# Output projection of the attention layer: three lumps of three products, or nine single products

## The chip, the cores and the metric

The kernel runs on one core of a Trainium2 chip. The metric is the device time of one execution in microseconds (us). The kernel before was timed three times: 6641.83, 6641.19 and 6638.29 us, a median of 6641.19. One further execution was profiled; it took 6638.09 us.

The engines are called TensorE (PE in the profile; PEld is its weight load), VectorE (DVE), ScalarE (ACT), GpSimd (POOL) and SyncE (SP, which issues nearly all DMAs).

## The reference

Four images of 384 channels and 64 x 64 pixels, all in fp32, pass two residual layers. The first is a selective state space layer (not touched here). The second is attention in which every pixel looks at a 7 x 7 window:

```python
qkv = einsum('oc,bchw->bohw', w_qkv, x) + b_qkv          # 12 heads of 32 channels
q, k, v = (qkv[:, 0] * scale, qkv[:, 1], qkv[:, 2])
logits = stack([sum_c q * k_pad[..., di:di+H, dj:dj+W] for di, dj in 7 x 7]) + rel_bias
attn = softmax(logits, axis=-1)
out = einsum('bnhwk,bnkchw->bnchw', attn, v_win).reshape(B, C, H, W)
out = einsum('oc,bchw->bohw', w_proj, out) + b_proj      # the output projection
x = x + out
```

The change concerns the last product alone, 384 x 384 weights on the 512 pixels of a stripe at a time.

## The kernel before

The state space layer fills the first 5145 us. While it runs, its idle engine time also makes keys, queries and values of the first images for the attention layer and stores them in DRAM (`kdr`, `qdr`, `vdr`). Which stripes have theirs is fixed when the program is built: stripes 0 to 14 have keys, queries and values, stripes 15 to 21 have values alone, stripes 22 to 31 nothing.

The attention layer (`attention_layer`, from line 1197) cuts each image into 8 stripes of 8 rows, 32 stripes in all. A stripe (512 pixels) is 12 units (`UNITS`): 4 pairs of 8 x 8 blocks, times 3 groups of four heads. The loop at line 1473 walks over the units `s` and writes out the work of four units in flight, in this order:

- what a piece of the unit before left over (`waiting`: mostly the eviction of its PSUM bank `mm`);
- `keep(s-4)`, every third unit: ScalarE copies a finished pair out of the bank `ov` into `aT`;
- `divide(s-1)`: reciprocal of the sums (`rs`, VectorE) and the product with it (`sg`, GpSimd);
- `scores(s)`: 8 products `lg` on TensorE into four banks, then for each head a bias-add with its row minimum on VectorE (`mx`) and an exponential on ScalarE;
- `turn(s-2)`: 8 transposes `pt` into two banks, one copied out by VectorE, the other by ScalarE (`pT`);
- the pieces of other stripes: keys, queries and values of stripe + 2 where they aren't in DRAM, and the output projection of stripe - 1 (`project`);
- `weigh(s-3)`: 16 products `ov` of the turned weights with the values `vw`.

After these come DMAs and small work: `load_res` at unit 0 (three loads of the residual into `o`), `load_keys` (three loads `kt`, one `q`) at unit 0, `surround` (four copies of key edges on GpSimd) at units 4, 6 and 8, and the values of a pair, four loads `vw`, after every third unit (2, 5, 8, 11).

Nothing is reordered: the class `Written` (lines 146 to 167) ties each engine's instructions to the order in which the program writes them, SyncE's DMAs included. Every engine and its queue goes through its list in order and waits on semaphores where data or a buffer isn't ready.

All pieces use the one bank `mm`. The projection (line 1334) makes the channel block `m` of a stripe by three products that add up in `mm`; in the unit after, VectorE adds bias and residual into `o` and SyncE stores it. `o` has three buffers, one per block: a load of the next residual block waits for the store of the block before it. Before the change, `pieces` (line 1366) puts the blocks at units 5, 7 and 9 of the following stripe.

In the profile one fp32 product shows as two passes (two MATMUL and two LDWEIGHTS rows).

Of the kernel before, what the change touches and what calls it, by code (L numbers as in the profile page):

```python
# [10 lines left out]
ALU = mybir.AluOpType  # L11
# [3 lines left out]
P = 128  # L15
C = 384
NJ = C // P
# [104 lines left out]
TX = 512  # L122
# [8 lines left out]
RB, CB = 8, 8  # L131
QB = RB * CB
NBLK = HW // CB
NPAIR = NBLK // 2
UNITS = NPAIR * NJ
# [35 lines left out]
def two_layers(  # L171
# [36 lines left out]
    for base, sign in ((0, 1), (GSZ - 1, -1)):  # L208
        nc.gpsimd.affine_select(
            out=grp,  # L210
# [9 lines left out]
    for base, sign in ((0, 1), (GSZ - 1, -1)):  # L220
        nc.gpsimd.affine_select(
            out=grpT,
# [974 lines left out]
    def attention_layer(eng, gm1, qkb, pjb, early, mv):  # L1197
        te, ve, se, ge, dq = eng
        scale = HD**-0.5
        stripes = NB * NXT  # L1200
        with ExitStack() as es:
# [5 lines left out]
            pjv = wt.tile([P, NJ], F32, name="pjv")  # L1207
            bias = early["bias"]
            w_pj = wt.tile([P, NJ, C], F32, name="w_pj")
# [10 lines left out]
            def ring(shape, tag, bufs, k):  # L1220

                if tag not in rings:
                    rings[tag] = list(early.get(tag, ()))
                    for i in range(len(rings[tag]), bufs):
                        rings[tag].append(sb.tile(shape, F32, name=f"{tag}{i}"))
                return rings[tag][k % bufs]

            def of(s):
                return s // NXT, s % NXT
# [11 lines left out]
            def at_of(s):  # L1241
                return ring([P, NJ, TX], "aT", 2, s)
# [45 lines left out]
            def load_keys(s, key_queue):  # L1288
                if s > 0:
                    load_stripe_keys(key_queue, kt_of(s), s)  # L1290
                    load_stripe_queries(dq, q_of(s), s)
# [34 lines left out]
            def o_of(s, m):  # L1326
                return ring([P, TX], "o", NJ, NJ * s + m)

            def load_res(s):
                b, r = of(s)  # L1330
                for m in range(NJ):
                    dq.dma_start(o_of(s, m), x1s[b][m * P : (m + 1) * P, r * TX : (r + 1) * TX])

            def project(s, m, ps):
                b, r = of(s)
                o = o_of(s, m)
                for j in range(NJ):
                    te.matmul(
                        ps, w_pj[:, j, m * P : (m + 1) * P],
                        at_of(s)[:, j, :].rearrange("p (b r c) -> p r b c", b=NBLK, r=RB),  # L1340
                        start=(j == 0), stop=(j == NJ - 1),
                    )
                yield
                ve.scalar_tensor_tensor(o, ps, pjv[:, m : m + 1], o, ALU.add, ALU.add)
                dq.dma_start(out[b, m * P : (m + 1) * P, r * TX : (r + 1) * TX], o)

            def output_bias(ps):

                for m in range(NJ):
                    for j in range(NJ):  # L1350
                        te.matmul(
                            ps[:, m : m + 1], w_pj[:, j, m * P : (m + 1) * P],
                            qkb[:, 2 * NJ + j : 2 * NJ + j + 1],
                            start=(j == 0), stop=(j == NJ - 1),
                        )
                ve.tensor_tensor(pjv, ps[:, :NJ], pjb, ALU.add)

            def has_values(s):
                b, r = of(s)
                return (b, NPAIR * r) in have_values  # L1360

            def has_keys(s):
                b, r = of(s)
                return (b, 2 * r) in have_keys and (b, 2 * r + 1) in have_keys

            def pieces(s, k):

                found = []
                t = s + 1
                if 0 <= t < stripes and not has_keys(t) and k == 0:  # L1370
                    found.append((query, t, 2))
                t = s + 2
                if 0 <= t < stripes:
                    if has_keys(t):
                        table = {}
                    elif has_values(t):
                        table = {2: (key, 0), 4: (key, 1), 6: (key, 2), 10: (query, 0), 11: (query, 1)}
                    else:
                        table = {
                            0: (value, 0), 1: (value, 1), 2: (value, 2), 3: (value, 3),  # L1380
                            4: (key, 0), 6: (key, 1), 8: (key, 2), 10: (query, 0), 11: (query, 1),
                        }
                    if k in table:
                        f, i = table[k]
                        found.append((f, t, i))
                t = s - 1
                if 0 <= t < stripes and k in (5, 7, 9):
                    found.append((project, t, (k - 5) // 2))
                return found

# [37 lines left out]
            def divide(u):  # L1428
                sg, sm, rs = sg_of(u), few_of("sm", u), few_of("rs", u)
                ve.reciprocal(rs, sm)  # L1430
                ge.tensor_tensor(sg, sg, rs.unsqueeze(2).broadcast_to([P, 4, NK]), ALU.mult)

            def turn(u):
                sg, pT = sg_of(u), pt_of(u)
                for c in range(NCH):
                    for hh in range(4):
                        te.transpose(
                            pts[c][:KN, hh * P : (hh + 1) * P],
                            sg[:, hh, c * KN : (c + 1) * KN], ident,
                        )  # L1440
                ve.tensor_copy(pT[:KN, 0, :], pts[0][:KN, :])
                se.copy(pT[:KN, 1, :], pts[1][:KN, :])
# [17 lines left out]
            def keep(u):  # L1460
                s, p, m = where(u)
                se.copy(
                    at_of(s)[:, :, p * P : (p + 1) * P],
                    ov[:, : NJ * P].rearrange("p (m q) -> p m q", m=NJ),
                )


            N = stripes * UNITS
# [1 line left out]
            last_stats = stats_phases(  # L1470
                (te, ve, se.activation, ge, lambda t: None), mv, gm1[NB - 1], lambda: mm, "b3"
            )
            for s in range(-3 * UNITS, N + 12):
                stripe, k = s // UNITS, s % UNITS
                for f in waiting:
                    next(f, None)
                waiting = []
                if s == 4:
                    output_bias(mm)
                if s > 4 and last_stats:  # L1480
                    last_stats.pop(0)()
                if 0 <= s - 4 < N and (s - 4) % NJ == NJ - 1:
                    keep(s - 4)
                if 0 <= s - 1 < N:
                    divide(s - 1)
                if 0 <= s < N:
                    scores(s)
                if 0 <= s - 2 < N:
                    turn(s - 2)
                mine = pieces(stripe, k)  # L1490
                for n, (f, t, i) in enumerate(mine):
                    ps = mm if s >= 0 else (mm, *lgs)[(s + n) % 5]
                    if n == 1 and 0 <= s - 3 < N:
                        weigh(s - 3)
                    g = f(t, i, ps)
                    next(g)
                    if n < len(mine) - 1:
                        next(g, None)
                    else:
                        waiting.append(g)  # L1500
                if len(mine) < 2 and 0 <= s - 3 < N:
                    weigh(s - 3)
                if k == 0 and 0 <= stripe - 1 < stripes:
                    load_res(stripe - 1)
                if 0 <= stripe + 2 < stripes and has_keys(stripe + 2):
                    if k == 0:
                        load_keys(stripe + 2, se if s < 0 else dq)
                    if k in (4, 6, 8):
                        surround(stripe + 2, (k - 4) // 2)
                t = stripe + 2  # L1510
                if 0 <= t < stripes and not has_values(t) and k in (6, 7, 8):
                    pad_values(dq, *of(t), k - 6)
                if k == 2 and 0 <= stripe + 3 < stripes and not has_keys(stripe + 3):
                    load_x(stripe + 3)
                if s == 3 - UNITS:
                    dq.dma_start(w_pj, proj_wT.rearrange("(k p) m -> p k m", p=P))
                if s == 2 * UNITS:
                    dq.dma_start(w_qkv, qkv_wT.rearrange("(k p) m -> p k m", p=P))
                if 6 <= k < 6 + NJ and 0 <= stripe + 3 < stripes and not has_keys(stripe + 3):
                    gn(stripe + 3, k - 6)  # L1520
                pair = (s + 1) // NJ + 1
                if (s + 1) % NJ == 0 and 0 <= pair < stripes * NPAIR:
                    load_pair_values(dq, vw_of(pair), pair)
# [3 lines left out]
    ]  # L1527
    dq = engines[-1]
    attention_layer(engines, *state_space_layer(engines))


# [44 lines left out]
```

## Time and profile before

| | |
|---|---|
| median of three executions | 6641.19 us (6638.29 to 6641.83) |
| the profiled execution, its own time | 6638.09 us |
| its span in the profile | 6636.4 us |
| attention layer, first score product to the end | 5145.1 to 6636.4 us |
| TensorE, VectorE, ScalarE, GpSimd busy in the span | 94%, 88%, 85%, 86% |
| stripes 2 to 12 (5219.27 to 5623.88 us): TensorE, VectorE, ScalarE, GpSimd busy | 386.2, 279.8, 324.1, 230.9 of 404.6 us |
| granted TensorE clock in these stripes | 1.00 |

The span is the time between the first and the last instruction of one execution; its own time holds a little around it. In the profile a line names the engine, the operation, the output tile, an arrow and the inputs (buffer numbers left out), shapes and a count. All lines bear L154, the line of the helper that writes the instructions, so groups are told apart by tile. A line of the view of waits names who waited, the releaser that came last, the total, how often and the longest. The ends of matmuls are modelled, so a high busy share of TensorE doesn't say that it has no idle time; starts are measured.

### The profile page before, as it was taken

The page shows a single profiled execution, that of the slowest core. Times are in us where ns is not written, and L with a number is a line of the kernel's source. Part 1 is how long each engine was busy: PE and PEld are TensorE (multiplying, and loading weights), DVE is VectorE, ACT ScalarE, POOL GpSimd, SP SyncE. Part 2 cuts the span into 40 slices and gives each one's busy share as a digit, 9 for nine tenths or more (in the row PEclk, how much of TensorE's full clock was granted, in tenths as well). Part 3 has the DMA queues.
Part 4 walks back from the last instruction along what each step waited for, and adds up shares of the span by engine and source line. Part 5 has one row for each costly group of instructions (what it writes and reads, how often), then busy time and mean ns, then how long its engine had stood idle before and what let it go on. Part 6 is the DMA issues. An engine that isn't in the chain of part 4 may idle for free.

```text
span 6636.4 us, 133738 instructions
## 1 busy us (share of the span) xinstructions
PE 6220.8 (94%) x47526; PEld 4267.2 (64%) x47526; DVE 5838.6 (88%) x10102; ACT 5612.0 (85%) x14147; POOL 5679.2 (86%) x3032
## 2 busy tenths in 40 slices
PE   6888888988999999999999999999997999999999
PEld 4666666666666666667666766676765555555555
DVE  4999999999999999999999999999998666555555
ACT  4888888888999999999999999999996778665556
POOL 3999999999999999999999999999999555444443
PEclk9999999999999999999999999999998999999999
DMA  5242423233444535353544434353533545223332
GB/s 187 89 131 89 137 91 131 84 130 101 148 153 131 164 119 166 121 174 118 168 133 139 151 124 153 123 166 120 167 110 92 172 151 158 95 94 108 102 101 93
DMA packets 783228, 859.99 MB, mean 130 GB/s; under 512 B 194976, under 2 KB 703024, under 8 KB 782384
## 3 DMA queue, kind: packets, MB, share of 16 engines
q1 hardware_dynamic: 779440, 850.65, 39.9%
q8 instruction: 377, 6.18, 0.4%
q14 instruction: 291, 2.38, 0.1%
q10 hardware_dynamic: 3120, 0.79, 0.1%
HBM read 745.54 MB, written 110.81 MB: 129 GB/s over the span
## 4 chain that ended last, share of the span: by engine, by line
DVE 32%; PE 32%; ACT 25%; issue 5%; POOL 4%; DMA 2%; SPq 0%; POOLq 0%; DVEq 0%; ACTq 0%
DVE h L154 28%; PE mm L154 19%; ACT da L154 8%; PE yps L154 5%; PE pt L154 4%; POOL h L154 3%; ACT sg L154 3%; ACT L154 3%; PE ov L154 2%; PE lg L154 2%; ACT dt L154 2%; ACT sz L154 2%; DVE xn L154 1%; DMA w_in<-wdr 1%; ACT pT L154 1%
## 5 line engine op out<-in xcount | busy, mean ns | idle before, releaser
L154 DVE TENSOR_TENSOR_SCAN h<-da,h 128x373 f32<-128x373 f32 (+1 forms) x4224 | 3616.5, 913 | 62.6 <-ACT da L154 54.0
L154 POOL TENSOR_TENSOR h<-h,BC 128x1488 f32<-128x1488 f32 (+1 forms) x1056 | 3259.8, 3104 | 45.0 <-ACT state L154 41.5
L154 ACT ACTIVATE da<-dt,nega 128x372 f32<-128x372 f32 (+1 forms) x4224 | 2378.9, 571 | 304.6 <-DVE h L154 270.8
L154 POOL TENSOR_TENSOR h<-dtx,BC 128x372 f32<-128x372 f32 (+6 forms) x1056 | 1756.2, 1684 | 42.7 <-ACT dtx L154 34.1
L154 PE MATMUL yps<-ident,h 128*124 128x128 f32 (+1 forms) x12672 | 1601.6, 279 | 121.7 <-POOL h L154 118.2
L154 PEld LDWEIGHTS yps<-ident,h 128*124 128x124 f32 (+1 forms) x12672 | 1456.1, 142 | 335.1 <-POOL h L154 211.5
L154 PE MATMUL mm<-xn,w_in 128*128 128x372 f32 (+3 forms) x3168 | 1091.6, 484 | 77.7 <-DMA w_in<-wdr 28.8
L154 POOL TENSOR_TENSOR sg<-sg,rs 128x784 f32<-128x784 f32 x384 | 574.1, 1495 | 638.3 <-DVE rs L154 510.9
L154 ACT ACTIVATE sg<-sg,mx 128x196 f32<-128x196 f32 x1536 | 685.2, 448 | 385.7 <-DVE mx L154 377.3
L154 DVE TENSOR_TENSOR h<-dtxps,BC 128x1488 f32<-128x1488 f32 (+6 forms) x792 | 967.3, 1235 | 1.3 <-ACT dtx L154 1.3
L154 PEld LDWEIGHTS mm<-xn,w_in 128*128 128x128 f32 x3168 | 571.7, 190 | 413.6 <-DVE h L154 56.8
L154 PE MATMUL mm<-xb,cw 128*128 128x372 f32 (+1 forms) x2112 | 700.1, 477 | 24.7 <-ACT xc L154 19.1
L154 DVE CUSTOM_DVE_ANT_0 sg<-lg,bias 128x196 f32<-128x196 f32 x1536 | 464.4, 358 | 179.7 <-PE lg L154 178.4
L154 PEld LDWEIGHTS mm<-xb,cw 128*128 128x128 f32 x2112 | 393.2, 189 | 287.9 <-ACT xc L154 38.9
L154 ACT ACT_TABLE_LOAD x441 | 565.8, 1283 | 8.4 <-PEq L1561 0.8
L154 PE MATMUL mm<-yg,w_out 128*128 128x372 f32 (+1 forms) x1584 | 526.8, 478 | 0.0
L154 PE MATMUL pt<-ident,sg 128*98 128x128 f32 x3072 | 446.8, 281 | 29.6 <-ACT pT L154 22.1
L154 PEld LDWEIGHTS pt<-ident,sg 128*98 128x98 f32 x3072 | 313.9, 128 | 182.3 <-issue 78.7
L154 PEld LDWEIGHTS mm<-yg,w_out 128*128 128x128 f32 x1584 | 289.0, 191 | 153.3 <-issue 2.3
L154 PEld LDWEIGHTS ov<-pT,vw 98*32 98x32 f32 x12288 | 189.6, 110 | 193.3 <-issue 136.0
L154 ACT ACTIVATION_READ_ACCUMULATOR sg<-sg,mx 128x1 f32 x1536 | 287.8, 187 | 0.0
L154 PE MATMUL mm<-xp,w_qkv 128*128 128x512 f32 x612 | 279.5, 593 | 0.0
(136 smaller groups left out, 7103.5 us busy)
## 6 DMA issues: line engine op xcount, KB each, us to landing
BC<-bcrows SPq DMA_DIRECT2D x320, 744.0 KB
w_in<-wdr SPq DMA_DIRECT2D x528, 192.0 KB
vw<-vdr SPq DMA_DIRECT2D x512, 147.0 KB
cw<-ddr SPq DMA_DIRECT2D x264, 256.0 KB
xs<-in_x_dram SPq DMA_DIRECT2D x210, 186.0 KB
wk<-in_qkv_wT_dram SPq DMA_DIRECT2D x180, 192.0 KB
o<-x SPq DMA_DIRECT2D x96, 256.0 KB
out_dram<-o SPq DMA_DIRECT2D x96, 256.0 KB
```

The lines of the kernel that those rows point to most:

```text
L154: ins = made(*args, **kw)
```

## The change

The new `project_part(s, i, ps)` makes one of the nine products of a stripe (block `i // 3`, term `i % 3`). Where it is the last term of its block, the eviction and the store follow in the next unit, as before. In `pieces` the nine parts go to units 3 to 11 of the following stripe, but only where the two stripes after it need no key, query or value products in this loop (they have keys in DRAM, or don't exist). Elsewhere `project` still runs whole at units 5, 7 and 9; it is now written by way of `project_part`. The stripes during which the new form is used are 1 to 12 and 31, and the tail after the last stripe. The loop is one step longer, so that the last eviction is written.

The eviction of the blocks moves from units 6, 8 and 10 to units 6, 9 and the next stripe's unit 0; the stores move with them. The third store then stands on SyncE behind the values of unit 11 and straight ahead of the residual loads of the next stripe.

```diff
+            def project_part(s, i, ps):
+
+                m, j = divmod(i, NJ)
+                te.matmul(
+                    ps, w_pj[:, j, m * P : (m + 1) * P],
+                    at_of(s)[:, j, :].rearrange("p (b r c) -> p r b c", b=NBLK, r=RB),
+                    start=(j == 0), stop=(j == NJ - 1),
+                )
+                yield
+                if j == NJ - 1:
+                    b, r = of(s)
+                    o = o_of(s, m)
+                    ve.scalar_tensor_tensor(o, ps, pjv[:, m : m + 1], o, ALU.add, ALU.add)
+                    dq.dma_start(out[b, m * P : (m + 1) * P, r * TX : (r + 1) * TX], o)
+
             def project(s, m, ps):
-                b, r = of(s)
-                o = o_of(s, m)
-                for j in range(NJ):
-                    te.matmul(
...
+                for j in range(NJ - 1):
+                    next(project_part(s, NJ * m + j, ps))
+                yield from project_part(s, NJ * m + NJ - 1, ps)
...
                 t = s - 1
-                if 0 <= t < stripes and k in (5, 7, 9):
+                if all(u >= stripes or has_keys(u) for u in (s + 1, s + 2)):
+                    if 0 <= t < stripes and k >= 3:
+                        found.append((project_part, t, k - 3))
+                elif 0 <= t < stripes and k in (5, 7, 9):
                     found.append((project, t, (k - 5) // 2))
                 return found
...
-            for s in range(-3 * UNITS, N + 12):
+            for s in range(-3 * UNITS, N + 13):
```

More of the change, by code (lines that the diff above doesn't have):

```diff
@@ L1332, in load_res @@
                     dq.dma_start(o_of(s, m), x1s[b][m * P : (m + 1) * P, r * TX : (r + 1) * TX])
-            def project(s, m, ps):
-                b, r = of(s)
-                o = o_of(s, m)
-                for j in range(NJ):
-                    te.matmul(
[L1339 to L1345, printed above, removed]
+            def project_part(s, i, ps):
[11 more added lines that the diff above has]
+                    dq.dma_start(out[b, m * P : (m + 1) * P, r * TX : (r + 1) * TX], o)
+            def project(s, m, ps):
+                for j in range(NJ - 1):
+                    next(project_part(s, NJ * m + j, ps))
+                yield from project_part(s, NJ * m + NJ - 1, ps)
             def output_bias(ps):
```

## The prediction

> **What bounds the kernel now.** The stretches by time came first: the last 1491 us of the 6636.4 us span, from 5145, are the attention stage, 32 stripes of 12 units. I took the start of the first score product (`lg`) of every unit. Stripes 2 to 12 last 36.74 to 36.76 us each (stripe 8: 37.12), stripe 1 37.23, stripes 14 to 19 about 50, 20 to 29 about 56.9. The diff touches the projections made during stripes 1 to 12, stripe 31 and the tail: elsewhere a following stripe still needs keys.
>
> TensorE's order of time in stripe 9 (start, length, engine, operation):
>
> ```profile
> 5481.95 0.60 PE L154 MATMUL lg<-kt,q 32*64 32x196 f32 x16
> 5482.48 1.38 PE L154 MATMUL pt<-ident,sg 128*98 128x128 f32 x8
> 5483.80 0.65 PE L154 MATMUL ov<-pT,vw 98*32 98x64 f32 x32
> 5484.38 0.60 PE L154 MATMUL lg<-kt,q 32*64 32x196 f32 x16
> ...
> 5489.44 0.60 PE L154 MATMUL lg<-kt,q 32*64 32x196 f32 x16
> 5489.98 1.39 PE L154 MATMUL pt<-ident,sg 128*98 128x128 f32 x8
> 5491.20 2.74 PE L154 MATMUL mm<-aT,w_pj 128*128 128x512 f32 x6
> 5493.87 0.65 PE L154 MATMUL ov<-pT,vw 98*32 98x64 f32 x32
> 5494.46 0.60 PE L154 MATMUL lg<-kt,q 32*64 32x196 f32 x16
> ```
>
> From `lg` to `lg` a plain unit takes 2.43 us, the first projecting unit 5.02 = 2.44 + 2.58. The 12 starts of a stripe are spaced 2.43, 2.62, 2.44, 2.43, 2.62, 5.02, 2.12, 5.13, 2.12, 5.13, 2.12, 2.56. So 2.12 us is what TensorE needs alone, when nothing it waits for is late, and 2.43 to 2.62 is what something else allows. The chain of waits says what:
>
> ```profile
> 5461.51 2.58 PE mm L154 x6
> 5464.08 0.58 PE ov L154 x32
> ...
> 5476.68 0.98 ACT sg L154 x4
> 5477.65 0.47 ACT pT L154
> 5478.12 0.38 ACT aT L154
> 5478.50 0.58 ACT sg L154 x3
> ```
>
> In projecting units the chain runs over TensorE; in plain units over ScalarE (exponentials, then a copy of the turned weights). The loop is: first bias-add on VectorE, 0.41 us later the first exponential, 1.78 us for four, reciprocal and next bias-add 0.24: 2.43. The waits of 5219 to 5624 us show both sides (columns: who for whom, total us, times, longest):
>
> ```profile
> ACT sg L154 <- DVE mx L154: 58.8, 35, 2.7
> ...
> PEld pt L154 <- ACT pT L154: 43.0, 99, 0.5
> ```
>
> ScalarE stands idle up to 2.7 us in 33 projecting units because TensorE is late; TensorE waits up to 0.5 us in 99 others because ScalarE is late. The two bounds alternate: each lump of 2.58 us stops ScalarE, and the time is not got back.
>
> **What the Trainium skill says.** "TensorE: Matmul & The Clock Gate" (Part 3, "What overlaps and what doesn't") has matmuls finish strictly in program order, so what stands behind a projection waits for it; the trace agrees: `ov` starts 0.95 us after the projection's last weight load, never earlier. "Perfetto Trace Analysis" (Per-instruction lifecycle) calls matmul ends estimates; the trace agrees (rows of 592 ns start 0.43 us apart), so I use starts alone. "PSUM — Partial Sum Buffer" (The four PSUM rules) says that a group's first product clears the flags of its whole bank: a group may stay open over three units only if nothing else starts one there; in these stripes `mm` has no other user. "DMA: Bandwidth & Descriptors" (Anatomy of one DMA) puts any wait of a transfer on the issuing sequencer; SP's own waits show this (100.9 us for `ov`, 69.7 for `rs`, up to 4.5 at once, in the same stretch), and it matters below.
>
> **The change part by part.** No product, eviction or DMA is added or removed: 9 products (18 passes), 3 evictions and 3 stores per stripe move.
>
> *The products.* Six passes cost 2.58 us where TensorE alone binds (4.70 = 2.12 + 2.58 in the units of stripe 15). Passes start 0.427 us apart, so 6 x 0.427 = 2.56 and at most 0.02 us belongs to entering and leaving the group. The value products (three of 384 columns) add 1.94 = 6 x 0.32 + 0.02: the same. One product: 2 x 0.427 + 0.02 = 0.87 us. The trace has no lone product between `pt` and `ov`; bounds of its fixed part: 0 (gone in overlap; not less, since the passes already stream without a gap) to 0.1 us (a further weight wait); I take 0.02.
>
> *Period of a unit with one product.* 2.12 + 0.87 = 2.99 us if nothing else binds. Checked against each engine: ScalarE's loop 2.43, with the `aT` copy 2.62: covered by 0.37. The second half of `pt` needs its bank freed by ScalarE's copy. With `lg` at 0, the bias-add starts at 0.71 (as after every projecting unit), exponentials end at 2.90, copy at 3.5; the next unit wants it at 2.99 + 1.03 = 4.0: 0.5 us of cover. POOL's multiply starts 0.5 after `lg`, lasts 1.5, is needed at 3.5. VectorE's eviction (0.75 us, queued ahead of reciprocal and bias-add) starts 0.5 us before the next `lg` and ends 0.27 after it, while the bias-add waits for `lg` until 0.71: free, and if that cover went, 3 x at most 0.3 us a stripe. The next group's first product waits for this eviction; it comes 1.66 after `lg`, so 1.4 us of cover.
>
> *A stripe.* Units 3 to 11 carry one product. Unit 0 follows a relaxed unit: 2.12. Unit 1: 2.54, the second after it, as 2.56 follows 2.12 now. Unit 2: 2.43. Unit 3, still on ScalarE's bound: 2.43 + 0.87 = 3.30; its product also needs the `aT` copy, which ends 1.60 after `lg` where the product wants 1.66: 0 to 0.1. Units 4 to 11: 8 x 2.99 = 23.92. Sum 34.31, against 36.75: 2.44 less.
>
> *All stripes.* Stripes 2 to 12 now sum to 404.63; 11 x 34.31 = 377.41: 27.2 less. Stripe 1 has no relaxed start: 2.56 + 2.62 + 2.44 + 3.30 + 23.92 = 34.84 against 37.23: 2.4. Stripe 13 begins after a relaxed unit: 0.4. Stripe 31: eleven units from 34.18 to 2.43 + 2.62 + 2.43 + 3.30 + 7 x 2.99 = 31.7, 2.5; unit 11's product there lies under the wait for the last exponentials, perhaps 0.1 more. The tail has the same order on every engine: 0. Sum 32.6 us.
>
> *SP.* The third store now falls after unit 11, straight before the loads of the next residual, and the load into the same buffer must wait until that store has landed; behind it in SP's queue stand the keys, the queries and the values. Now:
>
> ```profile
> 5476.69 3.19 SPq L154 DMA_DIRECT2D vw<-vdr  x4
> 5479.94 1.40 SPq L154 DMA_DIRECT2D o<-x  x3
> 5481.38 5.09 SPq L154 DMA_DIRECT2D kt<-kdr  x3
> 5486.51 0.78 SPq L154 DMA_DIRECT2D q<-qdr  x1
> ```
>
> The first key load is issued 4.5 us after the stripe's start and its sixteen completions are in at 10.8 (9.9 to 12.3 over the stripes). POOL copies from it in unit 4, at 12.7. After: store issued at 3.1, behind the values in the queues, landed at 7.5 to 8.4 (the residual load issued at 3.0 lands there now); key load at 8 to 9; landing, over queues that have emptied, some 3.3 us later: 11.5 to 12.5. POOL wants it at 10.4 (start of unit 4) + 2.0 = 12.4, and has another 2 us before its next multiply is missed by `pt`. Cost 0; to 1 us a stripe if landing takes as long as now (6.3: 15). Values asked for in unit 2 are needed in unit 9, 27.7 us after the start; now they are in by 18.5, so 4 us later does no harm, but in stripe 2, behind the 1.7 MB of `w_qkv`, they now land at 23.7: 0 to 2 us once. I take 0.6 in all.
>
> The sum, 32.0, is taken from the profiled execution: 6638.1 us, span 6636.4, to 6606.1 and 6604.4. The median of the runs shown is 3.1 us above that execution, so 6641.2 - 32.0 = 6609.
>
> **Rivals.** (a) *Part of it is eaten*: keys late on POOL by 1 to 1.5 us beyond its cover, or 0.1 us of fixed cost per product (9 x 0.08 = 0.7 us a stripe): 9 to 18 us lost, 6618 to 6627. For it: SP's queue is the one resource that gets a new wait. Against: the cover above. (b) *No change*: the product adds to ScalarE's period instead of filling its hole, 2.43 + 0.87 = 3.30 in all nine units; 9 x 3.30 + 7.1 = 36.8 a stripe, 6641. For it: the first projecting unit does just this (5.02). Against: after one such unit the wait is gone (2.12). (c) *Slower*: the new store-then-load wait. At 1:1 it must cost over 2.44 us a stripe to turn the sign, that is, key landing beyond 12.4 + 2 + 2.4 = 16.8, 6 us later than now. If the store's receipt took 8 us instead of 4.4 to 5.3, and the keys as long as now: landing near 18, 12 x 1.2 = 14 us slower, 6655. Against: stores on quieter queues land in 2.8 to 4.8 us. (d) *It gains more*: no waits are left on TensorE anywhere in these stripes: 12 x 2.12 + 9 x 0.87 = 33.3, 1 us a stripe better: 6597. Against: units 1 to 3 have no product to cover ScalarE.
>
> **How the numbers follow.** Forecast 77 in 100; (a) 12; (b) 4; (c) 4; (d) 3. The forecast's own range: fixed part 0 to 0.04, `aT` 0.1, `w_qkv` 0 to 2: 6605 to 6614. To leave no more than 2 in 10 outside it takes in half of (a): 6603 to 6621. A measurement of this kernel can tell about 0.2% (13 us) from no change: forecast, (d) and nearly all of (a) are faster, (b) the same, (c) slower: 0.91, 0.05, 0.04.
>
> **What would show it.** Starts of `lg` 2.99 us apart in units 4 to 11 of stripes 1 to 12, 3.30 in unit 3, 2.12 in unit 0; stripes of 34.3; ScalarE's waits on `mx` short and many instead of 2.7 us long; TensorE's waits on `pT` gone but for units 1 to 3; the key copies on POOL not waiting for DMA. Stripes 14 to 30 as before. It is wrong if the spacing is 3.3 (b), or if POOL waits for `kt` and the units after 4 stretch (a, c).

## The result, and the profile after

Median 6608.76 us (6603.49 to 6610.65, six runs) against 6640.41 for the kernel before (six runs in all): ratio 0.9952, 95% interval 0.9939 to 0.9965, so 32 us or about 0.5% faster. The forecast was 6609. The profiled execution took 6608.67 us, its span 6607.0 against 6636.4.

The span fell by 29.4 us. The attention layer, from its first score product to the end, fell from 1491.3 to 1459.3 us, by 32.0; the state space layer, in which the program is the same, happened to last 2.6 us longer in this execution (5147.7 us against 5145.1).

The spacing of the score products `lg`, unit by unit, in a stripe of the middle (stripe 9), worked out from the starts in the trace:

```
unit      0     1     2     3     4     5     6     7     8     9    10    11    stripe
before  2.44  2.62  2.43  2.44  2.62  5.01  2.12  5.12  2.12  5.13  2.12  2.56   36.75
after   2.12  2.55  2.44  3.29  2.99  2.98  2.98  2.98  2.98  2.98  2.98  2.99   34.27
```

TensorE's order of time in stripe 9 of the changed kernel (start, length, engine, operation) has one product (two passes) between the transposes and `ov` of every unit from 3 on:

```profile
5470.06 0.60 PE L154 MATMUL lg<-kt,q 32*64 32x196 f32 x16
5470.59 1.08 PE L154 MATMUL pt<-ident,sg 128*98 128x128 f32 x8
5471.50 1.02 PE L154 MATMUL mm<-aT,w_pj 128*128 128x512 f32 x2
5472.46 0.65 PE L154 MATMUL ov<-pT,vw 98*32 98x64 f32 x32
5473.04 0.59 PE L154 MATMUL lg<-kt,q 32*64 32x196 f32 x16
```

The eight transposes follow each other without a break (1.08 us; 1.38 in the plain units before, where the second four waited for ScalarE). The chain of work that ended last, in the same stripe, stays on TensorE from unit 4 on:

```profile
5471.66 0.86 PE mm L154 x2
5472.53 0.58 PE ov L154 x32
5473.11 0.53 PE lg L154 x16
5473.64 1.01 PE pt L154 x8
5474.65 0.86 PE mm L154 x2
```

The four pieces sum to 2.98 us, the unit's whole length. And the waits in stripes 2 to 12 (who for whom, total us, times, longest):

```profile
ACT sg L154 <- DVE mx L154: 50.2, 98, 1.0
...
PEld pt L154 <- ACT pT L154: 12.9, 33, 0.5
...
POOL kt L154 <- DMA kt<-kdr: 5.2, 9, 1.2
```

Before, ScalarE waited 35 times, up to 2.7 us, and the weight loads of the transposes waited for ScalarE 99 times, 43.0 us in all. Now ScalarE waits 98 times and never over 1.0 us, and the transposes wait for ScalarE 33 times, three a stripe. Counted by unit in stripes 2 to 11, they fall in units 1, 2 and 3 alone; before, they fell in units 0 to 5, 7, 9 and 11, that is, in all but those that follow a lump. The last line is new: GpSimd now waits for keys. It is followed up below.

### The profile page after: what moved, and what is told of

It reads as the page before. It is cut to its first block, busy times and chain, and to the rows that moved or that the text cites. A ratio compares the mean times of both kernels' runs of the same rounds, so it can differ in the third digit from the quotient of the medians.

```text
span 6607.0 us, 133726 instructions
## 1 busy us (share of the span) xinstructions
PE 6202.4 (94%) x47526; PEld 4262.0 (65%) x47526; DVE 5841.8 (88%) x10102; ACT 5612.8 (85%) x14147; POOL 5679.8 (86%) x3032
## 4 chain that ended last, share of the span: by engine, by line
PE 34%; DVE 32%; ACT 22%; issue 5%; POOL 4%; DMA 2%; SPq 0%; POOLq 0%; DVEq 0%; ACTq 0%
DVE h L154 28%; PE mm L154 19%; ACT da L154 8%; PE pt L154 5%; PE yps L154 5%; POOL h L154 4%; ACT L154 3%; PE ov L154 3%; PE lg L154 2%; ACT dt L154 2%; ACT sz L154 2%; ACT sg L154 2%; DMA w_in<-wdr 1%; DVE xn L154 1%; ACT xD L154 1%
## 5 line engine op out<-in xcount | busy, mean ns | idle before, releaser
L154 PE MATMUL pt<-ident,sg 128*98 128x128 f32 x3072 | 431.6, 280 | 14.0 <-ACT pT L154 8.5
```

Of the source, the lines that this page charges most:

```text
L154: ins = made(*args, **kw)
```

## The experiments

The theory: in these stripes TensorE needs 2.12 us a unit and ScalarE's loop 2.43 to 2.62. While TensorE works on the projection, ScalarE gets ahead, so that in the next unit TensorE doesn't wait for it: 0.31 to 0.50 us are saved, once. That holds for a lump (three products in one unit, 2.58 us) and for a single product (0.87 us) alike, so nine singles save nine waits a stripe and three lumps three. The rivals: the gain comes from the new places of evictions, stores and loads; each entry into a projection costs or saves something by itself; the new wait on SyncE eats part of the gain.

All stripe times below are medians of stripes 2 to 11, from the starts of `lg`. Each variant ran once, but for the one with halves, and the first layer, in which the program is the same, ended anywhere from 5143.9 to 5150.1 us; so the stripes decide, not the whole time.

### Lumps at the places of the change

```diff
-                    if 0 <= t < stripes and k >= 3:
-                        found.append((project_part, t, k - 3))
+                    if 0 <= t < stripes and k in (5, 8, 11):
+                        found.append((project, t, (k - 5) // 3))
```

> The changed kernel, but in the stripes concerned each output block is again made by three products in one unit, now at units 5, 8 and 11, so that evictions, stores and residual loads keep the places that the change gave them. Theory (a lump of 2.58 us stops ScalarE, single products fill TensorE's waits): units 5.0 us with a lump, 2.12 and 2.54 after it, about 36.5 us a stripe, nearly as before (36.75), time about 6638. Rival 1 (the gain comes from where VectorE's evictions and the stores went): about 34.3 us a stripe, as in the changed kernel, time about 6609.

Measured: 6640.46 us beside 6640.01 for the kernel before; 36.56 us a stripe. (About 6638 was expected; the attention layer started 3.0 us later than in the profile of the kernel before.) Stripe 9, TensorE:

```profile
5494.23 2.74 PE L154 MATMUL mm<-aT,w_pj 128*128 128x512 f32 x6
5496.90 0.65 PE L154 MATMUL ov<-pT,vw 98*32 98x64 f32 x32
5497.48 0.60 PE L154 MATMUL lg<-kt,q 32*64 32x196 f32 x16
...
5499.65 0.59 PE L154 MATMUL lg<-kt,q 32*64 32x196 f32 x16
...
5502.15 0.60 PE L154 MATMUL lg<-kt,q 32*64 32x196 f32 x16
```

After the lump one short unit (2.17 here, 2.12 as a rule), then 2.50, and ScalarE is the bound again. With evictions, stores and loads where the change has them, but lumps, 0.19 of the 2.48 us a stripe is gained. The first rival is out.

### Two and one

```diff
-                    if 0 <= t < stripes and k >= 3:
-                        found.append((project_part, t, k - 3))
+                    if 0 <= t < stripes and 5 <= k <= 10:
+                        found.append((project_two if k % 2 else project_part, t, (k - 5) // 2 * NJ + 2 * (1 - k % 2)))
```

`project_two` makes two products of a block in one unit.

> The nine products of a stripe as two and one, at units 5 and 6, 7 and 8, 9 and 10: six groups instead of three or nine. Theory: the unit with the first two products 4.16 us, later ones 3.85 (2.12 + 1.73), those with one 2.99, the unit after the last 2.12; about 35.6 us a stripe, that is, half of the gain, time about 6626. Rival 1 (places of evictions and stores, which differ by one unit from those before): about 36.7. Rival 2 (each entry into the projection has a fixed cost that the profile before did not show, so that more groups cost more): above 36.7 us.

Measured: 6627.51 us (before: 6640.01); 35.58 a stripe; the units from 5 to 11: 4.15, 2.99, 3.84, 2.98, 3.84, 2.99, 2.12. The expectation was met to 0.02 us. Six groups are not dearer than three: above TensorE's own 2.12 us, one product costs 0.86, two cost 1.72 and three 2.58 (4.70 = 2.12 + 2.58), so entering a projection has no cost that can be seen.

### Short exponentials, before and after

In both kernels:

```diff
-                        sg[:, hh, :], sg[:, hh, :], AF.Exp, scale=-1.0,
+                        sg[:, hh, KN // 2 : KN + KN // 2], sg[:, hh, KN // 2 : KN + KN // 2], AF.Exp, scale=-1.0,
```

The kernel before with this edit:

> The kernel before, with the exponentials over 98 of the 196 columns (the rest keep the biased logits: half of the softmax is left out), so that ScalarE's loop of a unit shrinks from 2.43 to about 2.13 us, close to TensorE's 2.12. Theory: plain units 2.12 to 2.35, and the lumps cost little more than their length: about 34.0 us a stripe in stripes 2 to 12. Rivals (a cost of the lumps that has nothing to do with ScalarE): the stripe is longer than the same kernel with single products by the full 2.4 us.

The changed kernel with it:

> The changed kernel with the same short exponentials (half of the softmax is left out). Theory: 33.4 to 33.6 us a stripe, units with a product still 2.98; the difference to the kernel before with short exponentials falls from 2.45 us a stripe to about 0.5, and in the whole time from 32 to about 6 us. Rivals: the difference stays 2.4 us a stripe.

Measured: 6593.35 and 6585.80 us. Stripes 33.97 and 33.44 us: the difference between lumps and singles fell from 2.48 to 0.53. The units of stripe 10, with short exponentials in both kernels:

```
unit      0     1     2     3     4     5     6     7     8     9    10    11    stripe
before  2.12  2.29  2.12  2.24  2.30  4.70  2.12  4.81  2.12  4.81  2.12  2.23   33.98
after   2.12  2.23  2.12  3.09  2.99  2.99  2.98  2.98  2.99  2.98  2.98  2.98   33.44
```

In the kernel before the plain units now take 2.12 to 2.30 and the lumps cost hardly more than their own length (2.12 + 2.58 = 4.70). TensorE's waits for ScalarE in stripes 2 to 12, 43.0 us there with whole exponentials, are nearly gone:

```profile
PEld pt L154 <- ACT pT L154: 5.6, 29, 0.2
```

The waits that the single products take away thus come from ScalarE's loop: where it is short, nearly all of the gain is gone. The whole time fell by 7.5 us from lumps to singles, not 6: 6.7 in the attention layer and 0.8 in the first layer, where the programs are the same. Both kernels have single long units; those of the changed kernel come next.

In the changed kernel with short exponentials, unit 6 of stripes 2, 7, 9 and 11 took 3.59 to 3.93 us where 2.98 was expected. GpSimd's order of time in stripe 7 shows why (in brackets the idle time before and what ended it):

```profile
5391.64 1.49 POOL L154 TENSOR_TENSOR sg<-sg,rs 128x784 f32<-128x784 f32 x1 [0.80 <-DVE rs L154]
5396.03 1.07 POOL L154 COPY kt<-kt 128x24 f32<-128x24 f32 x4 [2.90 <-DMA kt<-kdr]
5397.06 2.94 POOL L154 TENSOR_TENSOR sg<-sg,rs 128x784 f32<-128x784 f32 x2
```

The key edges waited 2.90 us for their load, and the two divisions behind them came late, the first of them too late for its transposes two units on. In the waits of stripes 2 to 12 of that kernel:

```profile
POOL kt L154 <- DMA kt<-kdr: 21.5, 11, 3.2
```

This is the mechanism of rival (c), at work where the units are shorter. The runs that follow take the wait on SyncE away.

### The residual loads at unit 2

```diff
-                if k == 0 and 0 <= stripe - 1 < stripes:
+                if k == (2 if 1 <= stripe - 1 < 12 else 0) and 0 <= stripe - 1 < stripes:
                     load_res(stripe - 1)
```

On the changed kernel:

> The changed kernel with the residual loads of stripes 1 to 11 issued at unit 2 instead of unit 0, so that no load stands behind the third store's landing and the keys and queries are issued some 4 us earlier. Theory (that wait is covered by GpSimd's slack): stripes 2 to 11 stay at 34.27 us; key copies on GpSimd no longer wait for a DMA (5.2 us in all in the changed kernel), and stripe 12, whose unit 8 took 3.76 us behind a late load of x, may come back to 34.3, at most 0.8 us in all; time 6607 to 6609. Rival (the third store's wait eats part of the gain): over 0.3 us a stripe better, below 6605.

On the changed kernel with short exponentials:

> The changed kernel with short exponentials (half of the softmax is left out) and the residual loads at unit 2. With short exponentials alone unit 6 of stripes 2, 7, 9 and 11 took 3.59 to 3.93 us instead of 2.98, after GpSimd had waited up to 3.2 us for keys. Theory (the wait of the residual load for the third store makes the keys late): all of units 4 to 11 at 2.98 to 2.99, GpSimd's wait for keys under 5 us in all (21.5 there), about 3 us faster than with short exponentials alone (6585.8), that is 6582 to 6584. Rival (keys late for another reason, such as values ahead of them in the queues): the long units stay.

Measured: 6609.09 and 6594.13 us. Both runs were spoilt in stripe 2: there the residual loads now stood behind the 1.7 MB of `w_qkv`, which the same queue fetches at unit 0, and VectorE's first eviction waited for them, 3.4 us in the first kernel (unit 6: 5.36 us) and 4.6 in the second (units 6 and 7: 8.01 and 4.16). The total expected of the second was missed by 10 us, most of it here and in a state space layer that was 3.0 us longer. In the first kernel stripe 0, which the edit doesn't touch, was 2.4 us longer too. In the other stripes both expectations hold, with one exception: the first kernel has 34.27 us a stripe, no wait of GpSimd for keys, and stripe 12 at 34.28 (35.04 in one profile of the changed kernel, but 34.27 in the other, so the edit need not be the reason). In the second, unit 6 of stripes 7 and 9 is back at 3.00 and 2.98, but that of stripe 11 still took 3.71, without a wait for keys, and the profile gives no reason for it.

### Keys first, then the residual loads

To part the two causes, the order at unit 0 alone was turned round:

```diff
-                if k == 0 and 0 <= stripe - 1 < stripes:
-                    load_res(stripe - 1)
...
                     if k == 0:
                         load_keys(stripe + 2, se if s < 0 else dq)
                     if k in (4, 6, 8):
                         surround(stripe + 2, (k - 4) // 2)
+                if k == 0 and 0 <= stripe - 1 < stripes:
+                    load_res(stripe - 1)
```

On the changed kernel:

> The changed kernel with only the order of two things on SyncE turned round at unit 0: keys and queries first, then the residual loads (with their wait for the third store). It is the test of the residual loads at unit 2 without their fault in stripe 2, where they stood behind 1.7 MB of weights. Theory (GpSimd's slack covers the keys' delay in the changed kernel): stripes 2 to 11 at 34.3 us as before, GpSimd not waiting for keys, stripe 2 without the 5.36 us unit; time 6606 to 6609. Rival (the wait costs something): 0.3 us a stripe or more better, below 6605.

With short exponentials:

> The same turn in the changed kernel with short exponentials (half of the softmax is left out), where GpSimd had waited for keys up to 3.2 us and unit 6 of four stripes took 3.59 to 3.93 us. Theory (those units are long because the keys stand behind the third store's landing): none of these stripes has a unit 6 over 3.1 us, GpSimd's waits for keys under 2 us in all; some 2.9 us faster than short exponentials alone (6585.8), 6582 to 6584. Rival: they stay long.

Measured: 6606.25 (before: 6637.87) and 6586.07 us. The first: 34.28 us a stripe, keys landed 8.6 to 9.9 us after the stripe's start instead of 12.1 to 13.5, no wait of GpSimd for them, and nothing gained in the stripes (343.5 us for stripes 2 to 11, with a unit of 3.41 in stripe 2; 342.8 and 343.0 in two profiles of the changed kernel). The new wait on SyncE costs the changed kernel next to nothing. The second: unit 6 at 2.98 or 2.99 in all stripes but stripe 4 (3.20), no wait for keys, stripes 2 to 11 334.6 us against 337.4. The late keys were what made those units long. Its whole time is no better than 6585.80, against the expectation: the state space layer was 2.7 us longer in its profile, which hides the 2.4 us that the attention layer gained.

### One product of three

```diff
             def project(s, m, ps):
...
+            def project_third(s, m, ps):
+                te.matmul(
+                    ps, w_pj[:, 0, m * P : (m + 1) * P],
+                    at_of(s)[:, 0, :].rearrange("p (b r c) -> p r b c", b=NBLK, r=RB),
+                    start=True, stop=True,
+                )
...
+                    if 0 <= t < stripes and k in (5, 8, 11):
+                        found.append((project_third, t, (k - 5) // 3))
```

> As the kernel with lumps at units 5, 8 and 11, but each block is made by one product of the three (two of three terms of the projection are left out in the stripes concerned). It measures what a lone product costs where ScalarE is the bound around it. Theory (the first product after plain units finds TensorE already waiting for ScalarE and adds its whole 0.87, and a part comes back in the unit after): units with a product 3.30, after it 2.12 and 2.54; about 31.3 us a stripe, 5.2 less than with lumps, which is twice 2.58, and not three times 1.72 less than singles. Rival (a product fills a hole wherever it stands): units with a product 2.5 to 2.99, about 30 us a stripe.

Measured: 6569.41 us; units with a product 3.30, those after it 2.12 and 2.55; 31.42 us a stripe, 5.14 less than with lumps: the six products left out cost 0.857 each. So a product of 0.87 us is not hidden by being short. Where ScalarE set the pace in the unit before, it adds all of its length (3.30 = 2.43 + 0.87); after it 0.31 comes back in the next unit and 0.07 in the one after that.

What it costs in all is worth working out. Three plain units take 7.49 us (2.43, 2.62 and 2.44 in the kernel before); with a lone product in the first they take 7.97 (3.30, 2.12 and 2.55): 0.48 more. The changed kernel has six products more in a stripe and takes 34.27, so these six cost 2.85, again 0.48 each. A product is no cheaper in a row of nine than alone. The second and third product of a lump are what is dear, 0.857 each.

The waits of the transposes for ScalarE (the line `PEld pt <- ACT pT`), counted by unit in stripes 2 to 11 of each kernel, show the rule behind this (each entry holds in at least nine of the ten stripes). A unit that carries a piece of the projection, whatever its length, is followed by a unit without that wait:

| kernel | units with a piece | units with that wait |
|---|---|---|
| before (lumps at 5, 7, 9) | 3 | 9: all but 6, 8, 10 |
| lumps at 5, 8, 11 | 3 | 9: all but 6, 9, 0 |
| one product at 5, 8, 11 | 3 | 9: all but 6, 9, 0 |
| two and one, 5 to 10 | 6 | 6: 0 to 5 |
| nine singles, 3 to 11 | 9 | 3: 1, 2, 3 |

Such a wait is worth about 0.38 us (7.49 / 3 - 2.12). What counts is thus in how many units the products stand.

### Halves over all twelve units

This says what is left: units 1 to 3, where TensorE still waits for ScalarE. The step takes products of 256 columns, one or two a unit, from unit 3 to unit 2 of the stripe after, for the outputs made during stripes 1 to 11; the output made during stripe 12 keeps its nine singles. The third residual load goes to unit 4, since its buffer is free only then, and stripe 30 gets single products too, where only unit 0 has another piece.

```diff
+            def project_half(s, n, ps):
+                m, r = divmod(n, 4)
+                h = r // 2
+                for j in (1, 2) if r % 2 else (0,):
+                    te.matmul(
+                        ps[:, h * TX // 2 : (h + 1) * TX // 2], w_pj[:, j, m * P : (m + 1) * P],
+                        at_of(s)[:, j, :].rearrange("p (b r c) -> p r b c", b=NBLK, r=RB)[
+                            :, h * RB // 2 : (h + 1) * RB // 2
+                        ],
+                        start=(j == 0), stop=(j == NJ - 1),
+                    )
...
+                if k < 3 and in_halves(s - 2):
+                    found.append((project_half, s - 2, k + 9))
+                if in_halves(t):
+                    if k >= 3:
+                        found.append((project_half, t, k - 3))
```

> A further step: in stripes 1 to 12 the nine products are cut into eighteen of 256 columns and spread over twelve units, one and two in turn, from unit 3 to unit 2 of the stripe after (outputs 0 to 10; output 11 as in the changed kernel); the third residual load moves to unit 4, behind its store; stripe 30 gets nine single products too. Theory (TensorE alone is the bound in every unit): units alternate 2.56 (2.62 at most, where ScalarE's copy of aT comes) and 2.99; 33.3 to 33.7 us a stripe against 34.27; stripe 30 2.4 us shorter; about 6597, some 12 us faster than the changed kernel. Rivals: weight loads of 0.19 us don't hide behind passes of 0.21 us (6 loads of 256 columns cost more than 3 of 512): 34.5 us a stripe or more, no gain; or ScalarE's loop still shows in the units of one product.

> The changed kernel itself, timed beside the kernel with halves on the same chip: 6604 to 6611, ratio 0.995 to the kernel before.

Measured on one chip, five runs each and nine of the kernel before: halves 6593.88 us (6593.13 to 6596.15), the changed kernel 6606.81 (6606.55 to 6609.57), the kernel before 6639.89. Ratios to the kernel before: 0.9931 (0.9919 to 0.9944) and 0.9952 (0.9938 to 0.9965). The halves are 12.9 us faster than the changed kernel, 12 were expected. Stripes of 33.28 us, which is TensorE's whole work there: 12 x 2.12 + 9 x 0.87 = 33.27. Their TensorE in stripe 9:

```profile
5448.92 0.60 PE L154 MATMUL lg<-kt,q 32*64 32x196 f32 x16
...
5450.36 1.03 PE L154 MATMUL mm<-aT,w_pj 128*128 128x256 f32 x4
...
5451.91 0.60 PE L154 MATMUL lg<-kt,q 32*64 32x196 f32 x16
...
5453.35 0.60 PE L154 MATMUL mm<-aT,w_pj 128*128 128x256 f32 x2
...
5454.46 0.59 PE L154 MATMUL lg<-kt,q 32*64 32x196 f32 x16
```

Units of 2.99 and 2.55 in turn: ScalarE's loop shows in neither, and of the 120 units of stripes 2 to 11 two have a transpose that waits for ScalarE. Stripe 12, which carries the last pieces of halves and nine singles, took 35.93. Two products of 256 columns take what one of 512 does (0.87), so the doubled weight loads (190 ns each) are hidden. Stripe 30 went from 38.7 to 36.6.

The series, all in us a stripe:

```
three lumps, units 5, 7, 9              36.75
three lumps, units 5, 8, 11             36.56
two and one, units 5 to 10              35.58
nine singles, units 3 to 11             34.27
eighteen halves, twelve units           33.28
TensorE's work alone                    33.27
```

## Why the prediction was right

*The bound.* That two bounds alternate, and that the singles take away waits for ScalarE, is shown: with short exponentials 2.48 us a stripe became 0.53, and lumps in the places of the change gained 0.19. Two readings were a little off. The time that a lump takes is in part got back, 0.31 us in the unit after it and 0.07 in the next. And TensorE's 99 waits are not those of "other" units than the projecting ones: units 5, 7 and 9 have them too, 6, 8 and 10 have not.

*The product.* 0.87 us, with 0.02 of fixed part: measured 2.98 - 2.12 = 0.86. The passes start 0.429 to 0.432 us apart in the trace of the kernel before, not 0.427, so six of them are the whole 2.58 and there is no fixed part to speak of. The product costs a third of three.

*The stripe.* Predicted 2.12, 2.54, 2.43, 3.30, 8 x 2.99, in all 34.31; measured 2.12, 2.55, 2.44, 3.30, 8 x 2.98, in all 34.27. The wait for the `aT` copy in unit 3 was nothing.

*All stripes.* For stripes 1 to 13, 31 and the tail the prediction took off 32.6 us and gave back 0.6 for the values of stripe 2; the attention layer became 32.0 shorter. That the two agree to a tenth is luck, since four small errors cancel; that they agree to about 1 us is not. The terms: stripes 2 to 12 27.2 predicted, 26.8 measured (404.61 to 377.79); stripe 1 2.4 against 2.1, because its unit 3 was 2.78 us long before where other stripes have 2.43, and the sum took 3.30 from the others instead of adding 0.87 to 2.78 (it took 3.65); stripe 13 0.4 against 0.4; stripe 31 with the tail 2.5 against 2.7. Stripe 12 has a unit of 3.76 in this profile, behind a load of `x` that came late; a second profile of the same kernel has not. Of the 0.6 for the values of stripe 2 nothing was seen: stripe 2 took 34.31.

*SyncE.* The third store's landing does hold the residual load up, as expected, 36.0 us in eleven stripes:

```profile
5462.74 0.41 SPq L154 DMA_DIRECT2D out_dram<-o  x1
5463.20 4.83 SPq L154 DMA_DIRECT2D o<-x  x3
5468.12 2.71 SPq L154 DMA_DIRECT2D kt<-kdr  x3
```

The first key load, issued 4.5 to 5.5 us after the stripe's start before, is now issued at 8.2 to 9.0 (predicted 8 to 9), and it landed at 12.1 to 13.5, on average 12.75 (predicted 11.5 to 12.5): it took 4.2 us to land where 3.3 was put. So one step was off: the prediction said that GpSimd would not wait for the keys; it waited nine times, 5.2 us in all. The cost was 0 all the same, because of the 2 us that GpSimd had behind it. In the second profile of the changed kernel the keys of stripe 7 came in at 14.4 us, and its unit 6 took 3.14 us instead of 2.98: the cover ended about where the prediction put it, at 14.4. The short exponentials show how thin the cover was: with keys in at 14.0 to 14.5 us after the stripe's start, and unit 4 starting 0.8 us earlier, 0.6 to 0.95 us of it came through in four stripes. The prediction's range for stores on quieter queues, 2.8 to 4.8 us, was too narrow: in stripes 2 to 12 of the kernel before, stores took 2.0 to 5.0.

*The rivals.* (b) is what the first product in a row and each lone one do in their own unit (3.30), and only they. (c) and the first half of (a) name a real mechanism; in the changed kernel it touched one stripe of its second profile, by 0.16 us. The second half of (a), a fixed cost per product, was not seen. (d) was ruled out for the change as made and is what the halves reach.

## What to carry to other kernels

Where two engines set the pace in turn, busy shares hide it: look at the start of one repeating instruction, unit by unit, and sort the units by what ended the wait. Work for the engine that waits should then be spread over as many units as it can be. Here each unit that carried a piece, short or long, alone or in a row, saved one wait of about 0.38 us; for the rest the products cost their full length. Moving a store ahead of a load into the same buffer puts a full DMA landing into the issuing queue; ask what stands behind it and how much slack its reader has, since the next speed-up will use that slack up.

## What the runs showed of the hardware

- An fp32 product with 128 x 128 weights on 512 columns costs 0.86 us where TensorE is the bound, two 1.72 and three 2.58; two products with 256 columns cost what one with 512 does, with twice the weight loads of 190 ns.
- The landing of the third 256 KB store took 4.7 to 5.4 us, median 5.0, in stripes 2 to 12 of the changed kernel, where it is issued right behind four value loads of 147 KB; in the kernel before, where it is issued some 3 us after the last of such loads, it took 2.0 to 3.7, median 2.2.
- With an identical program for the first layer, the start of the attention layer lay between 5143.9 and 5150.1 us over the thirteen profiles. A difference of a few us between two single runs of this kernel says nothing, while most stripes repeat to 0.02 us.
